# Conv attention and causal attention on one core: the order of one small DVE sum, the slots of some finishing steps, and another path for turning the values

## The chip, the cores and the metric

One core of one Trainium2 chip runs the whole program. The metric is the device time of one execution in microseconds. Engines are named as in the profile: PE (matmuls; PEld for its weight loads), DVE (vector), ACT (activations and copies), POOL, and SP, which here only issues DMAs.

## The reference, cut to what matters

Batches B = 4, channels C = 128, tokens N = 64 x 64 = 4096, everything in float32.

```
q, k, v = wq x, wk x, wv x                        (64 x 4096 each, per batch)
x = x + wo (softmax(k^T q) v^T)^T                 (layer 0: every token sees every token)
t = tokens of x                                   (4096 x 128, per batch)
t = t + softmax(causal(LN(t) Wq (LN(t) Wk)^T / sqrt(128))) LN(t) Wv       (layer 1)
t = t + scan(y = sigmoid(batchnorm(LN(t) W) + y V^T))
```

## The kernel before, in words

The kernel works on one batch after the other, first layer 0, then layer 1. A block is 512 query tokens, so each layer has 8 blocks per batch (`g` = 0 to 7). A block is cut into items, and an item covers two key tiles of 128 tokens: 16 items per block in layer 0, and 2g + 2 in layer 1, where later keys are masked. All items stand in one list, and one loop walks it. The loop's index `s` is called a slot here.

In each slot the loop writes, in this order: the scores of item s (PE into `s_ps`, L791 for layer 0 and L800 for layer 1), then Exp on ACT into one of four `p` buffers (L805 and L807); the values of item s - 2 (PE, `acc`, L851 and L859), so that PE has other work while Exp runs; the adding of `p` of item s to the block's denominators `dsum` (DVE, L831); and at most one due step out of a list `waiting`, or else one task out of a list `side`.

After a block's last item its denominators are added to one row (`den`, L875). In `folded` DVE turns 32x32 squares of it (L565) and sums them to `part` (L567). Four DMAs write `part` to DRAM (`by_token`, L579) and one reads it back by token (`own`, L580). For groups 0 and 1 of layer 1 and for the very last block a PE matmul does this in place of the DMAs. `project` sums the quarters of `own` (L586), takes the reciprocal (L587), multiplies `agg` by the output weights on PE (`o_ps`) and adds the scaled result to `xs` (DVE, L595). `normed` is the layer norm behind it (L604 to L611).

The steps after a block are chains: `finish0` for layer 0 and `finish1` for layer 1 yield (slots to wait, step). In layer 0 the fold comes one slot after the block's last item; the projection goes into the list `fill` and is taken from it at the last item of a later block. In layer 1 the chain is `sums`, `first` (projection and norm), `second` (DVE turns squares, and DMAs through DRAM, `by_c` and `xhT`, complete the turn), `third` (the matmul `wx_ps`, L727, which waits for `xhT`).

`keys(b, m)` gives the tasks which make the keys, queries and values of a batch: `cols0` (L513 to L519), `vals0` (the values by channels, L525, and an ACT copy `vT`, L529) and `vals0_by_tokens` (four PE transposes, L535, and an ACT copy, L537). For batches 1 to 3 they are put into `side` when group 1 of layer 1 of the batch before begins; for batch 0 they run at the start.

All DMAs of the main part are issued by SP, in order: a DMA that waits holds up those behind it. `ps_m` has two PSUM buffers for everything but scores and `acc`.

The order on each engine is not the order in which the text writes the instructions: a scheduler sorts them by priority and by estimated times, and adds the waits. `tc.keep_in_program_order` exempts one instruction from this on its engine.

Of the kernel before, what the change touches and what calls it, by code (L numbers as in the profile page):

```python
# [9 lines left out]
F32 = mybir.dt.float32  # L10
AF = mybir.ActivationFunctionType
ALU = mybir.AluOpType
AX = mybir.AxisListType
PSUM = bass.MemoryType.PSUM

P = 128
# [333 lines left out]
def fast_path(  # L350
# [113 lines left out]
    with tc.tile_pool(name="batch", bufs=1) as batch, tc.tile_pool(name="rows", bufs=2) as rowp, tc.tile_pool(  # L464
# [37 lines left out]
        def cols0(b, m):  # L502

            bt = bs[b]
            if m == 0:
                bt.kr = batch.tile([P, 2, N // 2], F32, tag="kr", name="kr")
                bt.swap = batch.tile([P, N // 2], F32, tag="swap", name="swap")
                bt.v = batch.tile([P, NT, M], F32, tag="v", name="v0")  # L510
            for h, w in enumerate((wqk, wkq)):
                ps = misc("kr_ps")
                nc.tensor.matmul(ps, lhsT=w, rhs=xs[:, b, ts(m + h * NB // 2, BLK)], start=True, stop=True)  # L513
                if h:
                    nc.scalar.copy(bt.kr[:, h, ts(m, BLK)], ps)
                else:
                    nc.vector.tensor_copy(bt.kr[:, h, ts(m, BLK)], ps)
                rows, keys = slice(M - h * M, P - h * M), slice(h * M, h * M + M)
                nc.sync.dma_start(out=bt.swap[keys, ts(m, BLK)], in_=bt.kr[rows, h, ts(m, BLK)])  # L519

        def vals0(b, m):

            ps = misc("v_ps")
            for h in range(2):
                nc.tensor.matmul(  # L525
                    ps[h * M : h * M + M], lhsT=wv0, rhs=xs[:, b, ts(m + h * NB // 2, BLK)], start=True, stop=True
                )
            vT = wk.tile([P, BLK], F32, tag="vT", name="vT")
            nc.scalar.copy(vT, ps)  # L529
            return vT  # L530

        def vals0_by_tokens(b, m, vT):
            ps = misc("vT_ps")
            for j in range(TPB):
                nc.tensor.transpose(ps[:, ts(j, P)], vT[:, ts(j, P)], ident)  # L535
            v = bs[b].v.rearrange("p (h t) c -> p t h c", h=2)[:, ts(m, TPB)]
            nc.scalar.copy(v, ps.rearrange("p (t h c) -> p t h c", h=2, c=M))  # L537

        def rows0(b, g):

# [42 lines left out]
        def project(layer, b, g, agg, own):  # L583

            rec = recs[:, layer, b, ts(g, TPB)]
            nc.vector.tensor_reduce(rec, own.rearrange("p q j -> p j q"), AX.X, ALU.add)  # L586
            nc.vector.reciprocal(rec, rec)  # L587
            op = misc("o_ps")
            for j in range(TPB):
                nc.tensor.matmul(  # L590
                    op[:, ts(j, P)], lhsT=agg[:, ts(j, P)], rhs=wv1 if layer else wo2, start=True, stop=True
                )
            for j in range(TPB):
                t = xs[:, b, ds(g * BLK + j * P, P)]
                nc.vector.scalar_tensor_tensor(  # L595
                    t, in0=op[:, ts(j, P)], scalar=rec[:, j : j + 1], in1=t, op0=ALU.mult, op1=ALU.add
                )
# [85 lines left out]
        def finish1(b, g):  # L683
            agg, den = bs[b].agg, bs[b].den
            mem = {}
            final = b == B - 1 and g == NB - 1

            def warm(n, rhs):

                ps = ps_s.tile([P, 2 * BLK], F32, tag="s", name="warm_ps")  # L690
                for _ in range(n):
                    nc.tensor.matmul(ps[:, : BLK // 2].rearrange("p (a c) -> p a c", c=P) if len(rhs.shape) == 3 else ps[:, : BLK // 2], lhsT=ident, rhs=rhs, start=True, stop=True)

            def first():
                if final:

                    nc.scalar.activation(spare, agg[:, 0:1], AF.Sigmoid)
                project(1, b, g, agg, mem["own"])
                if final:
                    warm(9, agg[:, : BLK // 2])  # L700
                nc.sync.dma_start(
                    out=x2[b, ts(g, BLK)].rearrange("(j p) c -> p j c", p=P),
                    in_=xs[:, b, ts(g, BLK)].rearrange("p (j c) -> p j c", c=P),
                )
                mem["xh"] = wk.tile([P, TPB, P], F32, tag="xh2", name="xh2")
                normed(b, g, mem["xh"])

            def second():
                mem["xhT"] = wk.tile([P, BLK], F32, tag="xhT2", name="xhT2")
                if final:  # L710
                    transposed(mem["xh"], mem["xhT"], "xh2T_ps", nc.vector.tensor_copy)
                    warm(1, mem["xh"][:, 2:])
                    return


                sq = squares(mem["xh"])
                by_c = dram2.tile([Q, S, Q, P], F32, tag="by_c", name="by_c")
                for q in range(Q):
                    nc.sync.dma_start(
                        out=by_c[:, :, q].rearrange("c r k -> r c k"),  # L720
                        in_=sq[ts(q, S)].rearrange("r c j t -> r c (j t)"),
                    )
                nc.sync.dma_start(out=mem["xhT"], in_=by_c.rearrange("c r q k -> (c r) (q k)"))

            def third():
                wp = misc("wx_ps")
                nc.tensor.matmul(wp, lhsT=wf, rhs=mem["xhT"], start=True, stop=True)  # L727
                if b == B - 1 and g == NB - 1:
                    in_range(True)
                nc.vector.bn_stats(ends[:, 3:] if final else stats[:, b * NB + g], wp)  # L730
                if b == B - 1 and g == NB - 2:
                    ahead()
                    in_range(False)

                to = xs[:, b, ts(g, BLK)]
                if final:
                    nc.scalar.copy(to.rearrange("p (s c) -> p s c", c=CPB), wp.rearrange("p (c s) -> p s c", s=STEPS))
                    warm(6, to[:, : BLK // 2])
                else:
                    nc.scalar.copy(  # L740
                        to.rearrange("p (s j q u) -> p s j q u", q=Q, j=TPB, s=STEPS),
                        wp.rearrange("p (q j u s) -> p s j q u", q=Q, j=TPB, s=STEPS),
                    )

            by_pe = final or g < 2

            def sums():
                mem["own"] = folded(den, by_pe)

            if by_pe:  # L750
                yield 1, lambda: (sums(), first())
            else:
                yield 1, sums
                yield 2, first
            yield 3, second
            yield 1 if final else 6 if g < 2 else 4, third


        class Item:
# [81 lines left out]
        def values(it):  # L841
# [4 lines left out]
            for h, (t, q0, n, o) in enumerate(it.at):  # L846
                if it.layer == 0:

                    for r in range(2):
                        part = slice(r * M, r * M + M)  # L850
                        nc.tensor.matmul(  # L851
                            bt.acc[h * M : h * M + M, r],
                            lhsT=bt.v[part, t],
                            rhs=it.p[part, o : o + n],
                            start=it.first,
                            stop=it.last,
                        )
                else:
                    nc.tensor.matmul(  # L859
                        bt.acc[:, 0, q0:],  # L860
                        lhsT=bt.xh[:, t],
                        rhs=it.p[:, o : o + n],
                        start=it.first and h == 0,
                        stop=it.last and h == 1,
                    )
# [19 lines left out]
        def keys(b, m):  # L885
            mem = []
            return [
                lambda: cols0(b, m),
                lambda: mem.append(vals0(b, m)),
                lambda: vals0_by_tokens(b, m, mem[0]),  # L890
            ]

        parts = [keys(0, m) for m in range(NB // 2)]
# [29 lines left out]
        for s in range(len(items) + SKEW + 16):  # L923
            if s < len(items):
                it = items[s]
                if it.first:
                    bs[it.b].rows = bs[it.b].next.pop(0)
                    if it.layer and it.g == 1 and it.b + 1 < B:
                        for m in range(NB // 2):
                            side += keys(it.b + 1, m)  # L930
                scores(it)
            if 0 <= s - SKEW < len(items):
                it = items[s - SKEW]
                values(it)
                if it.last:
                    rows()
                    tokens()
                    if fill:
                        fill.pop(0)(s)
                    push(s, (finish1 if it.layer else finish0)(it.b, it.g))  # L940
            if s < len(items):
# [178 lines left out]
```

## Time and profile before

| What | Value |
|---|---|
| Time, median of 3 runs | 2111.13 us (2109.12 to 2114.09) |
| Span of the profiled execution | 2112.6 us |
| PE busy | 2068.2 us |
| DVE busy | 1489.1 us |
| ACT busy | 1007.1 us |
| POOL busy | 117.9 us |
| DMA queue of SP, share of the 16 engines | 14.4% |

The span goes from the first to the last instruction of one profiled execution, on the clock of the chip. Busy time is time in which an engine executes instructions; waiting and issuing DMAs isn't counted. Matmuls are pipelined and their ends are modelled, so a PE that shows as busy isn't at its peak. In the waits, each line says which engine and line waited, then for whom, then the total in us, how often, and the longest. In a timeline each line has a start, a duration, the instruction, and in brackets the idle time before it with what ended it. In busy time by stretch, each engine has its busy us and its number of instructions; the granted clock of PE follows (1.00 is full speed), then the share of the DMA engines and GB/s.

### The profile page before, as it was taken

How to read it: one execution, taken by the hardware profiler on the slowest of the kernel's cores; microseconds unless marked ns; L12 is line 12 of the kernel's file. 1: busy time of each engine (PE TensorE's matmuls, PEld its weight loads, DVE VectorE, ACT ScalarE, POOL GpSimd, SP SyncE). 2: the span in 40 equal slices, each digit the busy share in tenths (PEclk: the TensorE clock that was granted, in tenths of full speed). 3: DMA queues.
4: the chain of work that ended last, by engine and by line, in shares of the span. 5: the costliest groups of instructions: out<-in, count | busy, mean ns of one | idle time of the engine just before them, and what ended most of it. 6: DMA issues, size and time to landing. Idle time of an engine off the chain costs nothing. (4 is left out here: it accounts for less than half of the span.)

```text
span 2112.6 us, 30728 instructions
## 1 busy us (share of the span) xinstructions
PE 2068.2 (98%) x11764; PEld 902.4 (43%) x11764; DVE 1489.1 (70%) x2853; ACT 1007.1 (48%) x1095; POOL 117.9 (6%) x221
## 2 busy tenths in 40 slices
PE   9999999999999999999999999999999999999998
PEld 3333354444333344444333335444433334544466
DVE  4888875545788896454688888544478988755568
ACT  5666633333665643333466653333356664333355
POOL 1000010000000011000000001000000001100000
PEclk9999999999999999999999999999999999999999
DMA  3110122100110112110011012110000111200044
GB/s 111 52 22 12 21 66 61 31 16 16 56 22 13 20 36 70 45 31 16 16 52 16 17 21 66 53 38 16 15 17 12 22 22 26 51 21 26 16 164 161
DMA packets 179499, 82.71 MB, mean 39 GB/s; under 512 B 114849, under 2 KB 163489, under 8 KB 178321
## 3 DMA queue, kind: packets, MB, share of 16 engines
q1 hardware_dynamic: 178336, 80.12, 14.4%
q8 instruction: 94, 1.54, 0.3%
q14 instruction: 61, 0.49, 0.1%
q0 software_dynamic: 288, 0.39, 0.1%
q10 hardware_dynamic: 720, 0.16, 0.0%
HBM read 42.69 MB, written 33.74 MB: 36 GB/s over the span
## 5 line engine op out<-in xcount | busy, mean ns | idle before, releaser
L831 DVE TENSOR_TENSOR dsum<-dsum,p 128x1024 f32<-128x1024 f32 x676 | 825.6, 1221 | 376.0 <-ACT p L807 292.4
L805 ACT ACTIVATE p<-s_ps,nshift 128x1024 f32<-128x1024 f32 x512 | 571.1, 1116 | 353.2 <-PE s_ps L791 271.8
L791 PE MATMUL s_ps<-kr 64*64 64x512 f32 x2048 | 530.6, 595 | 16.7 <-ACT p L805 16.7
L807 ACT ACTIVATE p<-s_ps 128x1024 f32<-128x1024 f32 (+2 forms) x288 | 274.2, 952 | 551.8 <-PE s_ps L800 521.0
L851 PE MATMUL acc<-p,v 64*64 64x512 f32 x4096 | 534.0, 592 | 1.7 <-ACT half L870 1.7
L791 PE MATMUL s_ps<-swap,kr 64*64 64x512 f32 x2048 | 530.6, 595 | 4.3 <-ACT p L805 4.3
L800 PE MATMUL s_ps<-rows,xhT 128*128 128x512 f32 (+3 forms) x1152 | 502.9, 559 | 0.0
L859 PE MATMUL acc<-p,xh 128*128 128x512 f32 (+3 forms) x1152 | 500.8, 557 | 0.0
L859 PEld LDWEIGHTS acc<-p,xh 128*128 128x128 f32 x1152 | 216.2, 190 | 244.3 <-issue 233.8
L800 PEld LDWEIGHTS s_ps<-rows,xhT 128*128 128x128 f32 x1152 | 213.4, 190 | 241.9 <-issue 208.4
L851 PEld LDWEIGHTS acc<-p,v 64*64 64x64 f32 x4096 | 155.3, 133 | 286.1 <-issue 272.7
L791 PEld LDWEIGHTS s_ps<-kr 64*64 64x64 f32 x2048 | 138.0, 133 | 157.5 <-issue 118.0
L791 PEld LDWEIGHTS s_ps<-swap,kr 64*64 64x64 f32 x2048 | 138.0, 133 | 143.6 <-issue 126.1
L458 POOL TENSOR_TENSOR ln_rstd<-ln_var,mhalf 128x4 f32<-128x4 f32 x64 | 69.7, 1090 | 1175.2 <-DVE ln_var L607 1147.6
L839 DVE TENSOR_TENSOR dsum<-dsum,p 128x256 f32<-128x256 f32 (+1 forms) x120 | 55.8, 498 | 58.0 <-POOL p L811 58.0
L595 DVE SCALAR_TENSOR_TENSOR xs<-o_ps,recs,xs 128x128 f32<-128x128 f32 x256 | 73.6, 344 | 7.0 <-PE o_ps L590 6.1
L611 DVE TENSOR_SCALAR xh<-xs,ln_mv,ln_rstd 128x128 f32<-128x128 f32 x256 | 71.7, 342 | 2.3
L811 POOL TENSOR_SCALAR_AFFINE_SELECT p<-p 128x128 f32<-128x128 f32 x128 | 40.4, 339 | 551.7 <-ACT p L807 546.0
L604 DVE BATCH_NORM_STATS2 ln_st<-xs 128x6 f32<-128x128 f32 x256 | 63.6, 270 | 0.0
L740 ACT COPY xs<-wx_ps 128x512 f32<-128x512 f32 x31 | 18.1, 585 | 85.7 <-DVE stats L730 85.7
L459 DVE TENSOR_TENSOR ln_z<-ln_rstd 128x4 f32<-128x4 f32 x64 | 10.5, 164 | 67.5 <-POOL ln_rstd L458 67.5
L829 DVE COPY dsum<-p 128x1024 f32<-128x1024 f32 x60 | 41.1, 684 | 18.7 <-ACT p L807 15.5
(137 smaller groups left out, 1046.7 us busy)
## 6 DMA issues: line engine op xcount, KB each, us to landing
xs<-in_xT SPq DMA_DIRECT2D x32, 256.0 KB, 3.1
by_r<-sqT SPq DMA_DIRECT2D x128, 64.0 KB, 2.2
xhT<-by_r SPq DMA_DIRECT2D x128, 64.0 KB, 2.0
x<-xs SPq DMA_DIRECT2D x32, 256.0 KB, 2.3
xr<-x SPq DMA_DIRECT2D x8, 1024.0 KB, 12.4
out_x<-xr SPq DMA_DIRECT2D x16, 512.0 KB, 5.1
by_c<-sqT SPq DMA_DIRECT2D x124, 64.0 KB, 1.8
xhT<-by_c SPq DMA_DIRECT2D x31, 256.0 KB, 2.6
```

Source lines behind the costliest of these rows:

```text
L458: nc.gpsimd.tensor_tensor(y, var, mhalf[:, : y.shape[-1]], ALU.pow)
L595: nc.vector.scalar_tensor_tensor(t, in0=op[:, ts(j, P)], scalar=rec[:, j : j + 1], in1=t, op0=ALU.mult, op1=ALU.add)
L604: nc.vector.bn_stats(st[:, j], xs[:, b, ds(g * BLK + j * P, P)])
L611: nc.vector.tensor_scalar(dst[:, j], xs[:, b, ds(g * BLK + j * P, P)], mv[:, j, 0:1], y[:, j : j + 1], ALU.subtract, ALU.mult)
L791: nc.tensor.matmul(ps[c * M : c * M + M, off : off + n], lhsT=bs[it.b].kr[part, h, ds(t % (NT // 2) * P + c * M, M)], rhs=rows[h], start=True,
L800: nc.tensor.matmul(ps[:, off : off + n], lhsT=lhsT, rhs=rhs, start=True, stop=True)
L805: nc.scalar.activation(it.p[:, :off], ps[:, :off], AF.Exp, bias=nshift)
L807: nc.scalar.activation(it.p[:, :off], ps[:, :off], AF.Exp, scale=float(P) ** -0.5)
L831: nc.vector.tensor_tensor(flat, flat, it.p, ALU.add)
L839: nc.vector.tensor_tensor(den[:, h, q0:], den[:, h, q0:], it.p[:, o : o + n], ALU.add)
L851: nc.tensor.matmul(bt.acc[h * M : h * M + M, r], lhsT=bt.v[part, t], rhs=it.p[part, o : o + n], start=it.first, stop=it.last,)
L859: nc.tensor.matmul(bt.acc[:, 0, q0:], lhsT=bt.xh[:, t], rhs=it.p[:, o : o + n], start=it.first and h == 0, stop=it.last and h == 1,)
```

## The change

The sum over the quarters (L586 before, L601 after) keeps its place in the program's order on DVE. In layer 1, `first` comes three slots after `sums` in place of two, for groups that fold by DMA. `third` comes six slots after `second` in place of four for group 7 of batches 0 to 2. A projection held in `fill` isn't taken at group 0 of layer 1. The keys' tasks of the next batch begin at group 3 in place of group 1. And for batches 1 to 3 the values are turned in another way: DVE transposes 32x32 squares straight out of PSUM into `sqv`, four DMAs write them to DRAM (`by_t`), and four read them back into `v`; the four PE transposes and the two ACT copies of such a block of values are gone. `v` is laid out with the two halves next to each other, for all batches.

```diff
-                bt.v = batch.tile([P, NT, M], F32, tag="v", name="v0")
+                bt.v = batch.tile([P, NT // 2, 2, M], F32, tag="v", name="v0")
...
+            if b:
+
+                sq = wk.tile([P, Q * TPB, S], F32, tag="sqv", name="sqv")
+                nc.vector.transpose(
+                    out=sq.rearrange("p (q j) r -> p q j r", q=Q), in_=ps.rearrange("p (j q t) -> p q j t", q=Q, t=S)
+                )
+                by_t = dram2.tile([S, Q, TPB, Q, S], F32, tag="by_t", name="by_t")
+                for c in range(Q):
+                    nc.sync.dma_start(out=by_t[:, :, :, c].rearrange("t q j r -> t (q j) r"), in_=sq[ts(c, S)])
+                for q in range(Q):
+                    nc.sync.dma_start(
+                        out=bs[b].v[ts(q, S), ts(m, TPB)].rearrange("t j h c -> t (j h c)"),
+                        in_=by_t[:, q].rearrange("t j c r -> t (j c r)"),
+                    )
+                return
             vT = wk.tile([P, BLK], F32, tag="vT", name="vT")
...
-            v = bs[b].v.rearrange("p (h t) c -> p t h c", h=2)[:, ts(m, TPB)]
-            nc.scalar.copy(v, ps.rearrange("p (t h c) -> p t h c", h=2, c=M))
+            nc.scalar.copy(bs[b].v[:, ts(m, TPB)], ps.rearrange("p (t h c) -> p t h c", h=2, c=M))
...
-            nc.vector.tensor_reduce(rec, own.rearrange("p q j -> p j q"), AX.X, ALU.add)
+
+            tc.keep_in_program_order(nc.vector.tensor_reduce(rec, own.rearrange("p q j -> p j q"), AX.X, ALU.add))
...
-                yield 2, first
+                yield 3, first
             yield 3, second
-            yield 1 if final else 6 if g < 2 else 4, third
+            yield 1 if final else 6 if g < 2 or g == NB - 1 else 4, third
...
-                            lhsT=bt.v[part, t],
+                            lhsT=bt.v[part, t % (NT // 2), t // (NT // 2)],
...
-                lambda: vals0_by_tokens(b, m, mem[0]),
+                lambda: b or vals0_by_tokens(b, m, mem[0]),
...
-                    if it.layer and it.g == 1 and it.b + 1 < B:
+                    if it.layer and it.g == 3 and it.b + 1 < B:
...
-                    if fill:
+
+                    if fill and (it.layer == 0 or it.g):
```

## The prediction

> **What bounds the kernel now.** I read the page first, then busy time by stretch, the waits, and last the timelines of single engines. The page says TensorE is busy nearly all the time:
>
> ```profile
> span 2112.6 us, 30728 instructions
> ...
> PE 2068.2 (98%) x11764; PEld 902.4 (43%) x11764; DVE 1489.1 (70%) x2853; ACT 1007.1 (48%) x1095; POOL 117.9 (6%) x221
> ```
>
> That leaves 44 us without a matmul, and it is an average over two kinds of stage. Busy time by stretch parts them (columns: busy us of PE, PEld, DVE, ACT, POOL, then granted clock and DMA share):
>
> ```profile
> 150.00:200.00 50.00, 48.55 (x447) 17.67 (x440) 45.46 (x65) 31.52 (x29) 1.01 (x1) 1.00 0.12 23
> 450.00:500.00 50.00, 50.00 (x129) 23.38 (x128) 24.67 (x45) 15.40 (x17) 2.08 (x5) 1.00 0.06 17
> 652.00:656.00 4.00, 2.04 (x20) 0.46 (x12) 3.76 (x10) 0.41 (x1) 0.00 (x0) 1.00 0.07 11
> 656.00:660.00 4.00, 3.24 (x16) 1.01 (x20) 3.69 (x4) 2.94 (x3) 0.00 (x0) 0.62 0.38 65
> 1548.00:1552.00 4.00, 1.24 (x12) 0.15 (x4) 3.69 (x4) 1.11 (x1) 0.00 (x0) 0.91 0.22 67
> 1552.00:1556.00 4.00, 3.54 (x10) 1.05 (x14) 1.18 (x2) 0.59 (x1) 0.00 (x0) 0.50 0.01 2
> 1556.00:1560.00 4.00, 4.00 (x32) 1.30 (x28) 1.23 (x1) 1.94 (x2) 0.00 (x0) 0.74 0.00 0
> ```
>
> Layer 1 (second row) is TensorE alone: 50 of 50 us, DVE half idle. Layer 0 (first row) is two engines at once: DVE 45.5 of 50 and PE losing 1.5. The other rows are two spots where PE stopped and its clock then fell. The waits say who holds whom:
>
> ```profile
> DVE dsum L831 <- ACT p L807: 292.4, 145, 3.7
> ...
> ACT p L805 <- DVE dsum L831: 67.8, 69, 4.1
> ...
> DVE recs L586 <- DMA own<-by_token: 40.9, 30, 3.7
> ...
> PE s_ps L791 <- ACT p L805: 21.0, 23, 2.7
> ...
> PE wx_ps L727 <- DMA xhT<-by_c: 6.3, 3, 3.2
> ```
>
> In layer 0 it is a chain: the sum of the quarters (L586) waits for its DMA, the `dsum` adds queue behind it on DVE, Exp (L805) waits for an add to free one of four `p` buffers, and PE waits for Exp. The timelines of DVE and of ACT show one case:
>
> ```profile
> 649.00 0.18 DVE L586 TENSOR_REDUCE recs<-own 128x4 f32<-128x16 f32 x1 [2.46 <-DMA own<-by_token]
> ...
> 654.32 7.83 DVE L831 TENSOR_TENSOR dsum<-dsum,p 128x1024 f32<-128x1024 f32 x6
> ```
>
> ```profile
> 655.60 1.11 ACT L805 ACTIVATE p<-s_ps,nshift 128x1024 f32<-128x1024 f32 x1 [4.07 <-DVE dsum L831]
> ```
>
> DVE idles 2.46 us though this block's result isn't needed for another 16 items; 6 us later Exp stands still for 4.07 us; and PE has idled 2 us in 652 to 656.
>
> **What the Trainium skill says.** "TensorE: Matmul & The Clock Gate", Part 1, has the PE clock halved after an idle window of about 3.4 us. The trace agrees in kind: 0.50 after the 3.21 us stop at 1549, 0.62 after the 2 us stop at 654. So a long stop costs more than itself: (0.09 + 0.50 + 0.26) x 4 = 3.4 us at 1548 to 1560, and 0.38 x 4 + 0.2 = 1.7 us at 656 to 664. The same page, Part 4, puts a transpose near 275 ns in a kernel; here a record is 272 to 276 ns too, but starts are 0.11 us apart, and the starts count. "VectorE: DVE Perf Modes", The three transpose paths, says that DVE turns 32x32 blocks only: hence the trip through DRAM. "DMA: Bandwidth & Descriptors", Two DMAs through the same engine are not ordered, wants a wait on the first transfer's completion before the read back; the trace shows such waits (L664 on `by_r`: 47.1 us in 51 waits on SP's own queue).
>
> **The change part by part.**
>
> A. *The pinned sum.* In the built order of before, L586 stands right after the norm of the block before, some 7 us behind its `part`; DMA needs about that (`by_token` issued from 642.00, sum released at 649.00). In the built order of after it stands behind the next block's `den`, about 28 us later, so it finds its data. Number of instructions and their durations stay. What is it worth? I take blocks by the start of their first Exp. PE's own pace is 16 items of 1.717 us, the spacing of Exp where nothing stalls, plus 1.25 us around the projection (one spacing of 2.97): 28.7 us. DVE's own pace, from `den` to `den`, is 29.2 us plus the wait of L586: 29.24 with a wait of 0.04 us, 30.30 with 1.09, 31.72 with 2.60. Per batch, blocks 0 and 1 run at PE's pace (DVE waits for Exp there, so nothing is gained). Blocks 2 to 7 took 179.1, 183.1, 182.2 and 179.5 us. Without the waits: 28.7 (PE still has its lead) + 4 x 29.15 + 30.4 for the last, which holds 1.66 us more PE work (spacings of 3.82 and 2.53 in place of 2.97 and 1.72), makes 175.7. The gain is 3.4 + 7.4 + 6.5 + 3.8 = 21.1 us, the clock's 1.7 us at 656 included. Check: the 40.9 us of waits less 9.7 in the four blocks 1, 6.9 in layer 1 and 2.2 in the blocks 0 is 22.1, of which PE's lead swallows some. The bounds: if PE's lead hid half of it, 10; if DVE's closer order shortened its pace to PE's, 0.4 x 16 = 6 more, 27.
>
> B. *Values by DVE and DRAM, batches 1 to 3.* Removed: 12 x 4 PE transposes. The PE timeline prices four at 0.44 us:
>
> ```profile
> 303.15 0.60 PE L535 MATMUL vT_ps<-ident,vT 128*128 128x128 f32 x4
> 303.59 0.59 PE L800 MATMUL s_ps<-rows,xhT 128*128 128x512 f32 x1
> ```
>
> 12 x 0.44 = 5.3 us, in layer 1, where PE is the bound, so all of it counts. Also removed: 24 ACT copies of 0.585 us, worth nothing, as ACT waits 521 us for scores in layer 1. Added: 12 DVE transposes out of PSUM.
>
> ```profile
> L625 DVE STREAM_TRANSPOSE sqT<-xh 128x512 f32<-128x512 f32 x63 | 44.8, 711 | 2.1
> ```
>
> That row reads SBUF; out of PSUM none is shown. DVE's 128x512 copy out of PSUM took 683 ns, against 692 for its SBUF add, so I take 0.71; up to 1.4 would be hidden as well, since DVE is idle for 25 of 50 us there (12 x 1.4 = 17 us at worst). Each holds one of two `ps_m` buffers until DVE comes to it; the built order puts it one to two adds after its matmul. Added on SP: 12 x 8 DMAs, priced by their kin:
>
> ```profile
> by_r<-sqT SPq DMA_DIRECT2D x128, 64.0 KB, 2.2
> xhT<-by_r SPq DMA_DIRECT2D x128, 64.0 KB, 2.0
> ```
>
> Issuing four `by_c` took 2.59 us on SP, so eight cost about 5.2 us, plus 2.2 us of waiting for the first four: 7.4 us of SP per block of values. The values are needed only when the next batch starts. What queues behind is `own<-by_token`, `xhT<-by_c` and the loads of tokens. The pinned sum in layer 1 now comes three slots after the fold (3.43 us each, 10.3 us) against the 7 us above; with SP held up, DVE may wait some us, and it has them. PE's cost: 0 expected, at most a stop as under the second rival.
>
> C. *Blocks put off.* In block 0 of batches 1 to 3 PE meets `wx_ps` of the last block of layer 1 before its `xhT` has landed: 1.54, 1.53 and 3.21 us. The third step goes from four slots to six, two slots of 1.72 us or 3.4 us, which covers all three. PE is the bound there, so 6.3 us return, and the 3.4 us of lost clock: 9.7. Lower bound 3, if transfers drift along. The first step's third slot moves its output, norm and DMAs by one slot for groups 2 to 7: nothing waits for them. The keys' later start (group 3) has 60 slots for 12 tasks; it moves their copies, `swap` DMAs and token loads with it, on engines with room. The held-back project at group 0 stands at the same place in both built orders: nothing.
>
> Sum: 21.1 + 5.3 + 9.7 = 36.1 us off the profiled span of 2112.6, so 2076.5. That execution lies 1.5 us above the median of the three runs, 2111.1, which makes 2075; I add 1 for waits that remain: 2076.
>
> **The rivals.** *PE's lead already hides A.* Then B and C alone remain: 2111 - 15 = 2096. For it: PE lost only 44 us in all, some 13 of them in the tail. Against it: DVE's blocks grow by the wait almost one to one, and Exp's idle gaps of 2.1 to 4.1 us stand right behind. *SP becomes the bound, and the kernel slower.* In the built order one `xhT<-by_c` of each turn is issued behind four `by_t`, which wait for DVE's transpose, which waits for `v_ps`; others stand behind `own` and token loads. If it lands late, PE stops at `wx_ps` in layer 1. A stop like that at 1549 costs 3.2 + 3.4 = 6.6 us; the gain of 36 is eaten by the sixth of some twelve, and nine give 2135. Against it: some 16 us of matmuls lie between that `v_ps` and that `wx_ps` in PE's order, and the chain needs about 8. *The edit does nothing*: true of the held-back project alone, not of A, whose place in the order differs.
>
> **How the numbers follow.** All three parts pay, 2066 to 2088: chance 0.74. A pays half or less, or new small waits: 2088 to 2106, chance 0.18. No change that a measurement can tell (0.2%, 4 us): 0.02. Slower through SP: 0.06. The range 2066 to 2094 leaves out about 0.1 to 0.2. Faster 0.92.
>
> **What would show it.** After: no wait of L601 for `own<-by_token` in layer 0; blocks near 29.2 us; Exp's idle gap behind DVE near 2.2 us once per block; no drop of clock before the tail; no wait of PE for `xhT<-by_c`; 48 transposes fewer and 5 us off the three layer-1 stretches with keys. A stop of PE at `wx_ps` in layer 1, or DVE waiting for `own` long enough to stall Exp, would prove me wrong.

## The result, and the profile after

| Kernel | Time, median of 6 runs (lowest to highest) | Span of the profiled execution |
|---|---|---|
| before | 2111.92 us (2109.12 to 2114.09) | 2112.6 us |
| after | 2074.72 us (2073.56 to 2076.93) | 2071.9 us |

The ratio is 0.9824, with a 95% interval of 0.9812 to 0.9837: 37.2 us faster, against 36.1 in the forecast's sum. The spans differ by 40.7 us. The time is always 1.7 us more than the span (2073.56 and 2071.9 belong to one execution, 2114.27 and 2112.6 to the other). So the profiled execution of before lay 2.4 us above its median and that of after 1.2 us below: 40.7 - 3.5 = 37.2.

The page of after, its first lines:

```profile
span 2071.9 us, 30792 instructions
...
PE 2052.6 (99%) x11716; PEld 894.6 (43%) x11716; DVE 1488.9 (72%) x2865; ACT 993.6 (48%) x1071; POOL 117.8 (6%) x221
```

PE has 48 matmuls fewer (12 x 4 transposes), and the time without a matmul is 19 us in place of 44. DVE is as busy as before. Busy time by stretch, with the columns as before:

```profile
150.00:200.00 50.00, 49.96 (x462) 18.26 (x456) 45.89 (x66) 33.08 (x30) 1.01 (x1) 1.00 0.13 23
450.00:500.00 50.00, 50.00 (x130) 23.42 (x129) 24.79 (x45) 15.19 (x17) 2.09 (x5) 1.00 0.07 17
```

In layer 0 (first row) PE now loses 0.04 us of 50 where it lost 1.5, and in the same 50 us it does 462 matmuls in place of 447. Layer 1 (second row) was and is PE alone. The waits:

```profile
DVE dsum L846 <- ACT p L822: 304.5, 150, 3.1
...
ACT xs L755 <- DVE stats L745: 72.0, 27, 4.4
DVE ln_z L459 <- POOL ln_rstd L458: 69.9, 64, 1.2
DVE dsum L846 <- ACT p L820: 54.3, 79, 2.0
...
ACT p L820 <- DVE dsum L846: 50.6, 69, 2.0
...
DVE sqv L531 <- PE v_ps L525: 4.2, 12, 0.4
```

And the waits of PE alone:

```profile
PE s_ps L806 <- ACT p L820: 1.8, 3, 0.6
```

The wait of the sum (L601) for `own<-by_token`, 40.9 us in 30 waits before, is gone from layer 0. Exp still waits for `dsum`, but 50.6 us in place of 67.8 and never more than 2.0 us in place of 4.1, and PE waits for Exp 1.8 us in place of 21.0. PE's wait at `wx_ps` for a DMA (6.3 us) has disappeared. The timeline of DVE shows where the sum went:

```profile
640.22 0.16 DVE L459 TENSOR_TENSOR ln_z<-ln_rstd 128x4 f32<-128x4 f32 x1 [1.12 <-POOL ln_rstd L458]
...
659.97 0.69 DVE L890 TENSOR_TENSOR den<-dsum 128x512 f32<-128x512 f32 x1
660.58 0.17 DVE L601 TENSOR_REDUCE recs<-own 128x4 f32<-128x16 f32 x1
660.69 0.71 DVE L579 STREAM_TRANSPOSE sq<-den 128x512 f32<-128x512 f32 x1
661.33 0.14 DVE L602 RECIPROCAL recs<-recs 128x4 f32<-128x4 f32 x1
661.44 0.69 DVE L581 TENSOR_REDUCE part<-sq 128x16 f32<-128x512 f32 x1
```

No wait stands at L601. It and the reciprocal now lie between `den`, `sq` and `part`, three steps of which each needs the one before.

One new thing was not forecast. The timelines of ACT and of PE in block 0 of batch 1:

```profile
543.01 0.59 ACT L755 COPY xs<-wx_ps 128x512 f32<-128x512 f32 x1 [3.27 <-DVE stats L745]
543.50 2.13 ACT L820 ACTIVATE p<-s_ps,nshift 128x1024 f32<-128x1024 f32 x2
```

```profile
539.35 1.12 PE L742 MATMUL wx_ps<-xhT,wf 128*128 128x512 f32 x2
...
544.67 0.65 PE L806 MATMUL s_ps<-swap,kr 64*64 64x512 f32 x2 [0.60 <-ACT p L820]
```

The third step's matmul finds its data and runs at 539.35. Its statistics on DVE (L745) queue behind `dsum` adds, and the copy on ACT (L755) waits for them, until 543.01. Two Exps stand behind the copy, though PE had finished the scores of the first by 541.5, and PE then misses an Exp for 0.60 us.

Stage lengths, by the start of the first Exp, show where the 40.7 us came from. Blocks 2 to 7 of layer 0 went from 179.14, 183.11, 182.19 and 179.45 us to 174.66 and three times 174.53: 25.6. Blocks 0 and 1 of batches 1 to 3 went from 60.86, 60.85 and 65.29 to 60.12 each: 6.6. Layer 1 with keys went from 260.62 to 259.01, three times: 4.8. The start gave 0.6, and the stretch behind the last layer 0 gave 3.0; of that 2.6 is the clock of the tail, which differs in the same way between two traces of after (experiments 9 to 12).

### The profile page after: what moved, and what is told of

It is laid out like the page before. It is cut to its first block, busy times and chain, and to the rows that moved or that the text cites. A ratio compares the mean times of both kernels' runs of the same rounds, so it can differ in the third digit from the quotient of the medians.

```text
span 2071.9 us, 30792 instructions
## 1 busy us (share of the span) xinstructions
PE 2052.6 (99%) x11716; PEld 894.6 (43%) x11716; DVE 1488.9 (72%) x2865; ACT 993.6 (48%) x1071; POOL 117.8 (6%) x221
## 3 DMA queue, kind: packets, MB, share of 16 engines
q8 instruction: 94, 1.54, 0.3%
## 4 chain that ended last, share of the span: by engine, by line
PE 82%; DVE 14%; issue 1%; ACT 1%; POOL 1%; DMA 0%; DVEq 0%; ACTq 0%; POOLq 0%
PE s_ps L815 22%; PE acc L874 22%; PE s_ps L806 14%; PE acc L866 14%; DVE dsum L846 9%; PE o_ps L605 2%; PE y_ps L1031 2%; PE r_ps L570 1%; PE wx_ps L742 1%; PE kr_ps L513 1%; ACT p L820 1%; PE v_ps L525 1%; DVE xr L1052 1%; POOL ln_rstd L458 1%; DVE xs L610 1%
## 5 line engine op out<-in xcount | busy, mean ns | idle before, releaser
L459 DVE TENSOR_TENSOR ln_z<-ln_rstd 128x4 f32<-128x4 f32 x64 | 10.4, 163 | 69.9 <-POOL ln_rstd L458 69.9
L755 ACT COPY xs<-wx_ps 128x512 f32<-128x512 f32 x31 | 18.1, 585 | 72.0 <-DVE stats L745 72.0
```

## The experiments

Experiments 1 to 4 shared one chip (before: 2109.31 us), 5 to 8 another (2109.58), 9 to 12 a third (2110.45). "Faster" is a difference of medians here; the ratio is another measure, and the two differ by up to 2.3 us (experiment 2: 6.1 by the medians, 8.4 by the ratio). Two theories stood at first: that each part is worth what the prediction says of it, and that PE's lead hides part A, so that the gain lies elsewhere.

**1. The pin alone, in the kernel before.**

```diff
-            nc.vector.tensor_reduce(rec, own.rearrange("p q j -> p j q"), AX.X, ALU.add)
+            tc.keep_in_program_order(nc.vector.tensor_reduce(rec, own.rearrange("p q j -> p j q"), AX.X, ALU.add))
```

> The kernel before with the pinned sum alone (A). My theory: DVE's waits for the quarters set the pace of layer 0's blocks 2 to 7, so nearly all of the 22 us in them come back: 21 to 25 us less than before, 2087 to 2091; no wait of L586 for its DMA in layer 0, blocks at 29.0 us. Rival (PE's lead hides the waits): less than 5 us, above 2107, although the waits are gone.

Measured: 2087.18 us, ratio 0.9887 (0.987 to 0.9904), 22.1 us faster. Blocks 2 to 7 take 174.4 to 174.6 us, as in after. One line of PE's waits is left of the stops:

```profile
PE wx_ps L727 <- DMA xhT<-by_c: 6.2, 3, 2.1
```

These are 2.13, 1.94 and 2.12 us, longer than two of the three in before (1.54, 1.53), and the granted clock is 0.87, 0.86 and 0.86 over the 12 us behind each, where it stayed 1.00 behind those two of before. So A works by itself, and it makes the stops that C removes dearer. The timelines of DVE in batch 1, of before and then of this kernel, show why `xhT` lands half a microsecond later with the pin:

```profile
524.54 0.18 DVE L586 TENSOR_REDUCE recs<-own 128x4 f32<-128x16 f32 x1 [0.58 <-DMA own<-by_token]
...
529.25 1.12 DVE L595 SCALAR_TENSOR_TENSOR xs<-o_ps,recs,xs 128x128 f32<-128x128 f32 x4
```

```profile
524.71 0.17 DVE L586 TENSOR_REDUCE recs<-own 128x4 f32<-128x16 f32 x1
...
525.20 1.13 DVE L595 SCALAR_TENSOR_TENSOR xs<-o_ps,recs,xs 128x128 f32<-128x128 f32 x4
```

The first Exp of the batch starts at 518.87 in before and at 514.32 here. So the scaled add of the last block comes 10.38 us after it in before and 10.88 here, where the sum and the reciprocal stand right ahead of it; the turn of the squares and the DMAs behind it come as much later. The stop of 3.21 us in before has another cause: there the last of the four `by_c` took 3.6 us to land, in place of 1.8 in the other two batches.

**2. The values by DVE and DRAM alone.** All edits of the diff that concern `v`, `sqv` and `by_t`, in the kernel before.

> The kernel before with the values of batches 1 to 3 by DVE squares and DRAM alone (B). My theory: 48 transposes of 0.11 us come off PE where PE is the bound: 5.3 us less, about 2106.6. Rival (SP's queue becomes the bound): slower than before by 6 us or more, with waits of PE for transfers in layer 1. Second rival (PE hides it): no change.

Measured: 2103.17 us, ratio 0.996 (0.9946 to 0.9975), 6.1 us faster, against 5.3 expected. The layer-1 stages with keys take 258.86 us in place of 260.62: 1.76 us each, exactly four times 0.44, so 5.3 for three batches.

**3 and 4. The slots alone.** First all slot edits without the pin and the values (with `yield 3, first`, `it.g == 3` and the hold-back at group 0), then only the third step's:

```diff
-            yield 1 if final else 6 if g < 2 else 4, third
+            yield 1 if final else 6 if g < 2 or g == NB - 1 else 4, third
```

> The kernel before with all steps that are put off (C), nothing else. As predicted, 9.7 us less (the stops at the layer-1 matmul in block 0 and the clock lost behind them), about 2102. The trace of after suggests less, 5 to 7 us, since Exp now waits behind the ACT copy of that matmul's result. If the slots matter only together with the pinned sum: 0 to 2 us.

> The kernel before with one number changed: six slots in place of four ahead of the third step of group 7. If that number carries C, it gives what all the slots give, within 1 us. If the later first step or the later keys carry part of it, it gives less, or even a longer stop since the transfers start no later.

Measured: 2107.29 us, ratio 0.9986 (0.998 to 0.9993), and 2105.58 us, ratio 0.9977 (0.9968 to 0.9986): 2.0 and 3.7 us by the medians, 3.0 (1.5 to 4.2) and 4.9 (3.0 to 6.7) by the ratios. The wait of PE for `xhT<-by_c` is gone in both, and all waits of layer 0 are there (the sum waits for `own` 44.2 us in the first). So the third step is all of C that pays, and alone it pays a third to a half of the 9.7 forecast.

**5. After without the pin.**

```diff
-            tc.keep_in_program_order(nc.vector.tensor_reduce(rec, own.rearrange("p q j -> p j q"), AX.X, ALU.add))
+            nc.vector.tensor_reduce(rec, own.rearrange("p q j -> p j q"), AX.X, ALU.add)
```

> The kernel after without the pin (A undone). My theory: the waits of the sum are back in layer 0 and cost 21 to 25 us, 2096 to 2100, as much as the pin gave alone. Rival (the parts lean on one another): well below 15 us or above 30.

Measured: 2096.84 us, ratio 0.9944 (0.993 to 0.9957), some 20 to 22 us slower than after. The wait is back at once, in DVE's waits:

```profile
DVE recs L601 <- DMA own<-by_token: 39.0, 29, 3.7
```

A is the largest part, and it is the pin, not the slots, that takes this wait away.

**6. After with the values on PE**, for all batches as for batch 0.

```diff
-            if b:
+            if b < 0:
...
-                lambda: b or vals0_by_tokens(b, m, mem[0]),
+                lambda: vals0_by_tokens(b, m, mem[0]),
```

> The kernel after with all values turned by PE and copied by ACT again (B undone). My theory: 48 transposes of 0.11 us are back on PE in layer 1: 4.8 to 5.5 us more, about 2080. Rival: no change, if PE's busy time there is only modelled and ACT or DVE sets the pace.

Measured: 2079.58 us, ratio 0.986 (0.9845 to 0.9875). Layer 1 with keys takes 260.77 us, 1.76 more than after. With experiment 2 this gives B from both sides: 5.3 us. The missing 0.5 us (4.8 in the trace) belongs to C's slots, which cost layer 1 about 0.15 us per batch (260.76 in experiment 3).

**7. A dose for DVE.** One more operation of an add's size (1.2 us) for DVE in each block of layer 0, behind the add of the item that starts with key tile 8. It takes the larger of `dsum` and `dsum`, and so changes no value.

```diff
+                if it.layer == 0 and it.tiles[0][0] == 8:
+                    nc.vector.tensor_tensor(flat, flat, flat, ALU.max)
```

> The kernel after with one extra DVE instruction per block of layer 0: the maximum of dsum with itself, 128x1024, which leaves its values as they are; some 1.33 us of DVE each, 32 of them. My theory (DVE sets the pace of blocks 2 to 7 at 29.0 us, PE only just below at 28.7): nearly each of 24 of them counts, less 1 to 2 us of lead per batch: 24 to 30 us more, about 2102. Rival (PE sets the pace and its lead hides DVE): under 5 us more.

Measured: 2103.07 us, ratio 0.9974 (0.9964 to 0.9984), 26.6 to 28.3 us slower than the two medians of after (2074.72, and 2076.49 in experiment 9). In the waits of ACT and of PE:

```profile
ACT p L820 <- DVE dsum L846: 66.9, 67, 3.6
```

```profile
PE s_ps L806 <- ACT p L820: 26.6, 23, 1.9
```

Blocks 5 and 6, which took 29.0 us, take 30.25 (one of the eight 30.63), so they grow by the dose itself. Blocks 3 and 4, at 28.72 us before (one 28.84), take 29.67 to 29.80 and 30.25 (one 30.61); block 2 stays at 28.72. So in blocks 5 and 6 of after DVE sets the pace, and 1 us of DVE costs 1 us there; the blocks ahead of them live on a lead that the dose uses up by block 3. The rival, that PE's lead hides DVE's time in all blocks, falls.

**8. The third step earlier.** One slot earlier than before had it, three in place of six.

```diff
-            yield 1 if final else 6 if g < 2 or g == NB - 1 else 4, third
+            yield 1 if final else 6 if g < 2 else 3 if g == NB - 1 else 4, third
```

> The kernel after with three slots in place of six ahead of the third step of group 7. PE meets that matmul 5.2 us earlier, some 3.7 us before its transfer lands, in three batches. Stop alone: about 3 x 3.7 = 11 us more, less the 3 us that Exp no longer waits behind the copy: 8 us. With the clock halved after a stop of that length, 2 to 3.4 us more per stop: 14 to 18 us, and a granted clock near 0.5 behind each stop.

Measured: 2087.68 us, ratio 0.9899 (0.9884 to 0.9914), 11 to 13 us slower than after by the medians, below the 14 to 18 expected; the spans differ by 14.6, within it. The timeline of PE, and the stretch behind the stop:

```profile
537.98 2.04 PE L742 MATMUL wx_ps<-xhT,wf 128*128 128x512 f32 x2 [3.59 <-DMA xhT<-by_c]
```

```profile
538.00:550.00 12.00, 12.00 (x82) 3.78 (x86) 5.67 (x6) 5.33 (x6) 0.00 (x0) 0.77 0.01 1
```

The three stops are 3.59, 3.63 and 3.80 us, 1.5 to 1.7 us (about one slot) longer than with the pin and four slots. The clock is 0.77, 0.86 and 0.86 over 12 us behind them, which is 2.8 + 1.7 + 1.7 = 6.2 us. Stops and clock make 17.2 us; off go 2.5 us which the late copy costs after (next experiment) and this kernel doesn't pay: 14.7 against the 14.6 measured.

**9 to 12. After once more, and what it still gives away.** After itself; then after with the copy ahead of the statistics:

```diff
-                nc.vector.bn_stats(ends[:, 3:] if final else stats[:, b * NB + g], wp)
+                if final:
+                    nc.vector.bn_stats(ends[:, 3:], wp)
...
                     nc.scalar.copy(
                         to.rearrange("p (s j q u) -> p s j q u", q=Q, j=TPB, s=STEPS),
                         wp.rearrange("p (q j u s) -> p s j q u", q=Q, j=TPB, s=STEPS),
                     )
+                    nc.vector.bn_stats(stats[:, b * NB + g], wp)
```

then after with the norm cut in two: the first half, up to the power on POOL, stays where it was, and the rest runs in the step that turns the squares, with its first multiply pinned in DVE's order as the sum is; then both.

```diff
-            rsqrt(y, var, stat.tile([P, TPB], F32, tag="z", name="ln_z"))
+            nc.gpsimd.tensor_tensor(y, var, mhalf, ALU.pow)
+            mem[:] = [mv, var, y]
+
+        def scaled(b, g, dst, mem, pin=False):
+            mv, var, y = mem
+            z = stat.tile([P, TPB], F32, tag="z", name="ln_z")
+            first = nc.vector.tensor_tensor(z, y, y, ALU.mult)
+            if pin:
+                tc.keep_in_program_order(first)
```

> The kernel after, unchanged, beside the three that build on it: 2074.7 as before, within 0.1%.

> The kernel after, but the third step copies its matmul's result on ACT first and takes its statistics on DVE afterwards. In the trace of after the copy waits 3.3 us for DVE's statistics in block 0 of batches 1 to 3, and Exp stands behind it; this costs about 1.2 us per batch. If that is the cause, 3 to 3.6 us less than after. If DVE then waits for ACT instead, or the copy wasn't what held Exp, no change.

> The kernel after, but in layer 0 the norm's second half comes in the next step, pinned behind two adds, so that DVE no longer waits 1.12 us per block for POOL. If DVE's pace still set blocks 3 to 6 of layer 0 (29.0 against 28.7 us), 2 us less than after in all, all blocks at 28.72. If PE's pace is reached already, no change.

> Both of these edits on the kernel after: the sum of the two, 5 to 5.6 us less than after, about 2069.4, if their stalls are separate ones.

| Kernel | Median | Ratio to before | Span |
|---|---|---|---|
| after again | 2076.49 us | 0.9836 (0.9823 to 0.985) | 2075.0 us |
| copy first | 2070.98 us | 0.9819 (0.9806 to 0.9832) | 2068.8 us |
| norm cut in two | 2071.66 us | 0.9818 (0.9805 to 0.9832) | 2070.0 us |
| both | 2068.83 us | 0.9807 (0.9794 to 0.982) | 2066.7 us |

The two medians of after, from two chips, lie 1.8 us apart. The traces show one source of it: in the tail, over 1992 to 2004, the clock is 1.00 in the first trace of after and 0.72 in the second, though both have the same stop of 1.41 us there. The drop can't come from that stop: it begins at 1991.84, and the stop at 1993.01. So sizes of 2 us are read from stage lengths here, not from medians.

With the copy first, ACT no longer waits for DVE at that place. Its timeline:

```profile
540.23 0.59 ACT L753 COPY xs<-wx_ps 128x512 f32<-128x512 f32 x1 [0.77 <-PE wx_ps L742]
541.28 1.12 ACT L822 ACTIVATE p<-s_ps,nshift 128x1024 f32<-128x1024 f32 x1 [0.46 <-PE s_ps L808]
```

Block 0 takes 31.16 us in place of 32.33, block 1 28.12 in place of 27.78: 0.82 us per batch, 2.5 in all. That is what the new wait cost, a little less than the 3 to 3.6 expected, as block 1 gives 0.34 us of it back.

With the norm cut in two, DVE works through POOL's power. Its timeline:

```profile
638.16 0.17 DVE L622 TENSOR_SCALAR ln_var<-ln_mv 128x4 f32<-128x4 f32 x1
638.24 2.55 DVE L862 TENSOR_TENSOR dsum<-dsum,p 128x1024 f32<-128x1024 f32 x2
640.71 0.15 DVE L631 TENSOR_TENSOR ln_z<-ln_rstd 128x4 f32<-128x4 f32 x1
```

The 1.12 us of idling at L459 have gone, two adds stand in their place, and blocks 2 to 6 all take 28.72 us, PE's pace; Exp's waits for `dsum` in layer 0 (50.6 us) have left the list. That is worth only 2.2 us in all, as PE's pace lies just 0.3 us under DVE's 29.0. Both together take 4.7 us off the layer-0 stages (238.37 and three times 233.24 us), the sum of the two, so their stalls are separate ones. This version is the fastest measured: its runs (2068.33 to 2070.83 us) all lie below every run of after.

## Why the prediction was right

The forecast of 2076 us was met within 1.3 us, and the signs and the order of the parts hold. That it came so close is partly luck: in the traces A gave 4.5 us more than its term, C 3.1 less and B 0.5 less, and these nearly cancel. One reading was wrong and changes nothing: the 1.5 us by which the profiled execution lay above the median compares its span with times. Its own time, 2114.27 us, lay 3.1 us above 2111.13; the median less 36.1 is 2075 either way.

**A was right in mechanism, and a little larger than forecast.** Forecast 21.1 us; 22.1 alone in timed runs, 20 to 22 by taking it out, 25.6 between the two traces. Two terms were mis-sized. The first is DVE's pace without waits: 29.0 us, not 29.15. The working counted the sum and the reciprocal in that pace as before, where they held DVE for 0.2 us (in one block of before without a wait the sum starts at 679.08 and the next instruction at 679.17, the reciprocal at 680.40 and the next at 680.51). In their new place they cost nothing. In block 0 they don't stand there; DVE's timeline of the copy-first kernel has one such block:

```profile
543.86 0.69 DVE L892 TENSOR_TENSOR den<-dsum 128x512 f32<-128x512 f32 x1
544.59 0.71 DVE L579 STREAM_TRANSPOSE sq<-den 128x512 f32<-128x512 f32 x1
545.33 0.69 DVE L581 TENSOR_REDUCE part<-sq 128x16 f32<-128x512 f32 x1
```

From the start of `den` to that of `part` it is 1.47 us, and with the two between, in the timeline of after above, 1.47 us too (659.97 to 661.44): they lie in gaps that the dependent steps leave anyway. It is so in the whole trace of after: `den` to `part` is 1.5 us in 28 blocks with the two between and in 24 without. The 0.15 us in four blocks of four batches make 2.4. The second is PE's lead, which makes the other 2.1: it lasts for three blocks per batch, 2 to 4 (28.72 each; 28.84 for block 4 of batch 0), not for one.

**B was right**: 5.3 us forecast, 5.3 by experiments 2 and 6. The price was the spacing of PE's starts (0.44 us for four), not the length of a record (0.27 us each, which would have given 13; the figure near it that the prediction quotes from "TensorE: Matmul & The Clock Gate", Part 4, is for bf16, and these are float32). DVE's transposes out of PSUM had no row before; after has one:

```profile
L531 DVE STREAM_TRANSPOSE sqv<-v_ps 128x512 f32<-128x512 f32 x12 | 8.6, 717 | 4.2 <-PE v_ps L525 4.2
```

717 ns, against the 0.71 us taken from the row that reads SBUF.

**C was right on what it removes, and missed what it adds.** Forecast 9.7; the three blocks 0 of before exceed 31.16 us, the length without any stop, by 1.6 + 1.6 + 6.0 = 9.2. But the moved step puts a DVE and an ACT instruction at a new place too, and there the copy waits for statistics behind adds: 2.5 us back, 6.6 net. The prediction followed the step on PE and on SP and not on DVE and ACT. And of the 9.2, 4.5 come from the one stop of 3.21 us and its clock, one slow transfer taken for a rule. In the trace of experiment 2 the three stops are 1.39, 1.60 and 1.51 us, and blocks 0 and 1 exceed 59.28 us, their length without a stop, by 4.6 us in three batches. With the slots alone (experiment 3) they exceed it by 1.3, and layer 1 takes 0.4 more: a gain of 2.9 us, in keeping with the 3.0 of the ratio. With the pin the slots are worth more, since the stops are then 2 us long and cost clock each time: blocks 0 and 1 exceed 59.28 us by 11.3 in experiment 1 and by 2.5 in after, 8.7 us less. The timed runs agree: between experiment 1 and after, B and C make 13 us (ratios 0.9887 and 0.9824), and B is 5.3 of it.

**The held-back project**: nothing, as forecast. The order built on PE, DVE, ACT and SP is the same with and without it.

**The rivals.** That PE's lead hides A is refuted by experiments 1, 5 and 7. That SP becomes the bound is refuted by the trace of after: PE never waits for `xhT<-by_c`, the sum (L601) never waits for `own`, in layer 1 either, and layer 1 became shorter.

**The clock.** The prediction put the lost clock behind the stop of 1549 at 3.4 us; block 0's length gives 6.0 - 3.2 = 2.8. The clock fell at 1551.29, and PE stood still until 1552.46, so 0.6 of the 3.4 lie in the stop itself and were counted twice. And the stop at 654, which it calls 2 us, was 2.7.

## What to carry to other kernels

Read waits stage by stage, and ask what stands behind the waiter in its own queue: here a 0.17 us sum, placed just ahead of its DMA's landing, cost 20 us, because DVE had no spare time in that stage and its adds release Exp's buffers. When a step is moved to be ready later, follow every instruction that it issues, on each engine: C cured PE's wait and made one on ACT. A part's worth can depend on the others: in blocks 0 and 1 the slots gained 3.3 us alone (4.6 less 1.3) and 8.7 behind the pin, because the pin lengthened the stops that they cure. The timed runs are too coarse to show this in the sum: the ratios of the three parts alone multiply to 0.983, and all together gave 0.9824. And ask of a long stop in one trace whether it comes again in the next one.

## What the runs showed of the hardware

"TensorE: Matmul & The Clock Gate", Part 1, of the Trainium skill puts the drop of the clock behind an idle window of about 3.4 us. Here shorter stops lowered it too, and where a stop lay in time mattered as much as its length. Busy time by stretch around the first stop in experiment 1 (536.48 to 538.60) shows one drop:

```profile
535.36:538.77 3.41, 1.28 (x13) 0.35 (x6) 3.20 (x3) 1.12 (x1) 0.00 (x0) 1.00 0.24 77
538.78:542.19 3.41, 3.41 (x13) 0.70 (x16) 2.01 (x3) 0.59 (x1) 0.00 (x0) 0.50 0.00 0
542.20:545.61 3.41, 3.41 (x36) 1.14 (x32) 1.47 (x2) 2.23 (x2) 0.00 (x0) 1.00 0.00 0
```

The clock is 0.50 for 3.41 us, which costs 1.7 us, and 0.86 over 12 us is the same drop seen from afar. The changes of the clock in a trace lie on a grid of 3.413 us. In before it fell or rose at 657.00, 660.41, 1551.29, 1558.12, 2029.16 and 2035.98: the distances are 1, 261, 2, 138 and 2 steps of 3.413. The 52 changes in the 14 traces all fit such a grid within 0.01 us, each trace having its own, and a drop for a stop lasts one step or two.

Ahead of the tail the clock fell nine times. Each time PE had stood still for 1.94 to 2.72 us within the grid step that had just ended. Of the steps at full clock none with up to 1.86 us of it was followed by a drop (two had 1.86, in experiment 7), and one with 2.00 us wasn't either (experiment 4, part of a stop of 3.03 us). So the steps have the length of the page's window, but PE need not stand still for all of one. And a stop of 2.72 us lowered the clock in before, where it lay within one step, and another of 2.72 us didn't in experiment 5, where the edge of a step at 710.90 parted it into 1.07 and 1.65. In the tail this doesn't hold: there the clock fell in three traces behind a step with 1.4 us of standing still, and why is open.
